# Half of a gated layer's weights through DMA transposes, and a reciprocal shared by two batches from the first group on

## The chip, the cores and the metric

The kernel runs on one core of a Trainium2 chip. The metric is device time in microseconds (us) of one execution. Before the change three runs took 1891.08, 1893.07 and 1893.68 us; the median is 1893.07.

## The reference

Two layers are computed on x (64 batches, 128 steps, 512 features) in 32-bit floats. Layer 0 is a gated recurrence without a matrix in its loop; layer 1 is a GRU whose 128 steps follow one another, conditioned on a vector for each batch.

```python
# layer 0
f = sigmoid(x @ W_f.T + b_f);  i = sigmoid(x @ W_i.T + b_i)
total = f + i + 1e-8;  f, i = f / total, i / total
new = i * (x @ W_h.T + b_h)
lc = cumsum(log(f + 1e-8))          # over time
hidden = cumsum(exp(lc[-1] - lc_before) * new) + exp(lc) * cond
x = x + hidden
# layer 1: gates z and r, state h, with C_* applied to cond
x = x + gru(cond, x)
```

W_f, W_i and W_h are 512 x 512 and are used transposed: the contraction runs over their columns.

## The kernel before, in words

**Groups and chunks.** Layer 0 takes the 64 batches in 16 groups g of four (512 columns: 4 batches of 128 steps), and the 512 outputs in four chunks c of 128 partitions. The loop at L1038 goes over (g, c). For each chunk `chunk_products` (L280) calls `gate` (L219) three times, n = 0, 1, 2 for W_f, W_i, W_h. A gate is four matmuls of 128x512 (L232), one for each 128 of the contraction, into one of two PSUM banks of its kind. ScalarE applies the sigmoid to the first two (L285, L291). VectorE then does the rest of the chunk: `chunk_total` (L319) adds f and i, `chunk_shares` (L322) divides by that sum, `chunk_new` (L374), `chunk_retained` (L385) and `chunk_summed` (L379) are a product and scans over time. The steps of a chunk end within the next one: `chunk_rest` (L400) puts `chunk_weighted` (L393) and `chunk_initial` (L398) of the chunk before behind the sum of the present one, and on GpSimd (POOL) `chunk_first` (L312), `sums_of_chunk` (L278) and `add_hidden` (L253). `add_hidden` also stores the new x to DRAM, as x2d (L261, on the SP queue). `add_eps` (L308) is one more step on ScalarE, between VectorE's L349 and its scans.

**The division.** In group 0 VectorE takes the reciprocal of all 512 sums of a partition (L328). In later groups the reciprocal is shared: batches are paired, the product of two sums is formed (L335, `r`), its reciprocal taken (L337, half as many elements), and multiplied with the other sum of the pair (L339, `over`). `r` and `over` lie in the two PSUM banks of the tag "tp".

**Weights of layer 0.** They come as rows, 12 pieces of 128 outputs by 512 (`load_w_rows`, L91, one for each chunk c and kind n) into `w_rows`. TensorE turns each piece with four transposes (L190) into a "tp" bank, and ScalarE copies it (L191) into W0. The pieces of chunks 0 and 1 are turned while chunk (0,0) runs; in chunks 1 and 2 the three pieces of the following chunk are turned one by one between the gates (`chunk_products`, `w0_transposed`).

**x.** Group 0's x comes as rows and is transposed on TensorE. For later groups another way is used. A float is two 16-bit halves. `x_halves` (L152) issues DMAs that transpose 16-bit elements from DRAM into the tile `held` (L155): the two halves of a float end up in neighbouring partitions. `x_words` (L160) sends them from there, in four DMAs on SP of 64 KB (L166), into a tile `words`, where both halves of a number lie in the same partition. `x_joined` (L171) is one ScalarE copy (L177) that interleaves the halves into xT. There are four sets of words for each group, (u, m) = (0,0), (0,1), (1,0), (1,1), and two `words` buffers (tag "x", which `cond_sb` uses first). The sets of group g+1 are sent and joined during group g, and xT of a group is needed from its first gate on.

**After chunk (1,0)** `conditioning` (L444) loads the three conditioning weights C_r, C_z and C of layer 1 into the tile `cw` (L428, 1 MB each, on SP), which takes the place of `w_rows` (tag "wa"), and multiplies them with the transposed cond (`pv`, 64 matmuls at L473, in both "tp" banks). They stand behind chunk (1,0)'s last gate on TensorE. `bias1` is filled by twelve small DMAs (L448). Layer 1's other weights, w_s and w_x (L435), are loaded in pieces.

**What sets the order.** Instructions passed to `pin` keep the order of the program on their engine: all matmuls, ScalarE, VectorE and POOL work around the change. The DMAs on SP are not pinned; a scheduler places them when the kernel is built, and SP then takes its queue in that order, waiting at each DMA for what it needs. ScalarE's joins, copies and sigmoids are one queue in program order.

Of the kernel before, what the change touches and what calls it, by code (L numbers as in the profile page):

```python
# [10 lines left out]
U16 = mybir.dt.uint16  # L11
# [4 lines left out]
P = 128  # L16
# [3 lines left out]
def kernel(  # L20
# [38 lines left out]
    nc = tc.nc  # L59
    B, S, D = x.shape  # L60
    K = D // P
    GB = 4
    NG = B // GB
# [12 lines left out]
    work = ctx.enter_context(tc.tile_pool(name="work", bufs=1))  # L76
    psum = ctx.enter_context(tc.tile_pool(name="psum", bufs=2, space=PSUM))

    def pin(instruction):
        return tc.keep_in_program_order(instruction)  # L80
# [8 lines left out]
    w_rows = wpool.tile([P, K, 3, D], F32, tag="wa", name="w_rows")  # L89

    def load_w_rows(c, n):  # L91
        nc.sync.dma_start(w_rows[:, c, n, :], (W_f, W_i, W_h)[n][c * P : (c + 1) * P, :])

    x_rows = {}

# [46 lines left out]
    def by_batch(t):  # L142
        return t[:, 1:NP].rearrange("p (b t) -> p b t", t=S1)[:, :, :S]
# [6 lines left out]
    words = {}  # L150
# [20 lines left out]
    def x_joined(g, u, m):  # L171

        if u == m == 0:
            xT[g] = work.tile([P, K, NT], F32, tag="xt", bufs=2, name=f"xT_{g}")
        to = xT[g][:, m * K // 2 : (m + 1) * K // 2, u * NT // 2 : (u + 1) * NT // 2]
        pin(
            nc.scalar.copy(  # L177
                to.bitcast(U16).rearrange("p k (n h) -> p k n h", h=2),
                words.pop((g, u, m)).rearrange("p k h n -> p k n h"),
            )  # L180
        )
# [4 lines left out]
    def transposed(dst, rows, n=P, m=K, copy=nc.scalar.copy):  # L186

        tp = psum.tile([P, m, n], F32, tag="tp", name="tp")
        for k in range(m):
            pin(nc.tensor.transpose(tp[:, k, :], rows[:, k * P : (k + 1) * P], ident[:n, :n]))  # L190
        pin(copy(dst, tp))  # L191
# [11 lines left out]
    W0 = wpool.tile([P, K, 3, K, P], F32, tag="wb", name="W0")  # L203

    xT = {}

    def w0_transposed(c, n, copy=nc.scalar.copy):
        transposed(W0[:, c, n], w_rows[:, c, n, :], copy=copy)

# [9 lines left out]
    def gate(g, c, n):  # L219
        p = psum.tile([P, NT], F32, tag=f"p{n}", name=f"p{n}_{g}_{c}")  # L220

        blocks = [slice(0, NT)]
        if (g, c, n) == (0, 0, 0):
            copies = (nc.vector.tensor_copy, nc.scalar.copy)
            blocks = [slice(tb * P, (tb + 1) * P) for tb in range(K)]
            w0_transposed(0, 0)
            for tb in range(2):
                x_transposed(0, tb, copy=copies[tb % 2])
        for tb, tokens in enumerate(blocks):
            for k in range(K):  # L230
                pin(
                    nc.tensor.matmul(  # L232
                        p[:, tokens],
                        lhsT=W0[:, c, n, k, :],
                        rhs=xT[g][:, k, tokens],
                        start=(k == 0),
                        stop=(k == K - 1),
                    )
                )
            if len(blocks) > 1 and tb + 2 < K:  # L240
                x_transposed(0, tb + 2, copy=copies[tb % 2])
            elif len(blocks) > 1 and tb + 2 == K:
                transposed(biasT, bias0, n=3 * K, m=1)
                w0_transposed(0, 1)
        return p.rearrange(f"{layout(g)} -> p b t", b=GB)
# [34 lines left out]
    def chunk_products(g, c):  # L280

        f, i = fs[c % 2], is_[c % 2]
        fb, ib = by_batch(f), by_batch(i)
        p = gate(g, c, 0)
        pin(nc.scalar.activation(fb, p, AF.Sigmoid, bias=biasT[:, 0, c : c + 1]))  # L285
        if g == 0 and c == 0:
            w0_transposed(0, 2)
        elif g == 0 and c + 1 < K:
            w0_transposed(c + 1, 0)
        p = gate(g, c, 1)  # L290
        pin(nc.scalar.activation(ib, p, AF.Sigmoid, bias=biasT[:, 0, K + c : K + c + 1]))  # L291
        if g == 0 and c == 0:
            transposed(condT, cond_sb, n=B)
            w0_transposed(1, 0)
        elif g == 0 and c + 1 < K:
            w0_transposed(c + 1, 1)
        if g + 1 < NG:
            for u, m in ((), ((0, 0), (0, 1)), ((1, 0),), ((1, 1),))[c]:
                x_joined(g + 1, u, m)
        p = gate(g, c, 2)  # L300
        if g == 0 and c + 1 < K:
            for n in range(1 if c == 0 else 2, 3):
                w0_transposed(c + 1, n)
        return p

    def add_eps(c):
        fb = by_batch(fs[c % 2])
        pin(nc.scalar.activation(fb, fb, AF.Copy, bias=EPS))  # L308
# [13 lines left out]
    def chunk_shares(g, c, meanwhile):  # L322

        h = hidden[g, c]
        hb = by_batch(h)
        if g == 0:
            meanwhile()
            pin(nc.vector.reciprocal(h, h))  # L328
            over = hb
        else:  # L330
            r = psum.tile([P, NT], F32, tag="tp", name=f"r_{g}_{c}")[:, : NT // 2]
            over = psum.tile([P, NT], F32, tag="tp", name=f"over_{g}_{c}")
            pairs = hb.rearrange("p (a b) t -> p a b t", a=2)
            r_ = r.rearrange("p (b t) -> p b t", t=S)
            pin(nc.vector.tensor_tensor(r_, pairs[:, 0], pairs[:, 1], ALU.mult))  # L335
            meanwhile()
            pin(nc.vector.reciprocal(r, r))  # L337
            pin(
                nc.vector.tensor_tensor(  # L339
                    over.rearrange("p (a b t) -> p a b t", a=2, t=S),  # L340
                    pairs[:, ::-1],
                    r_.unsqueeze(1).to_broadcast([P, 2, GB // 2, S]),
                    ALU.mult,
                )
            )
            over = over.rearrange("p (b t) -> p b t", t=S)
        both = fi[c % 2][:, :, 1:NP].rearrange("p n (b t) -> p n b t", t=S1)[:, :, :, :S]
        pin(
            nc.vector.tensor_tensor(  # L349
                both, both, over.unsqueeze(1).to_broadcast([P, 2, GB, S]), ALU.mult  # L350
            )
        )
        add_eps(c)
# [684 lines left out]
    for g in range(NG):  # L1038
        for c in range(K):
            last = g == NG - 1 and c == K - 1  # L1040
            if g + 1 < NG and c == 0:
                x_halves(g + 1, 0)
                x_halves(g + 1, 1)
            elif g + 1 < NG and c < K - 1:
                x_words(g + 1, c - 1, 0)
                x_words(g + 1, c - 1, 1)
            p = chunk_products(g, c)
            meanwhile = chunk_rest(g, c)
            if last:
                meanwhile()  # L1050
                break
            chunk_shares(g, c, meanwhile)
            if g > 0:
                load(4)

            if g >= 2 and (c == 0 or c == 2 and g >= 14):
                subtracts(early_differences, 1)
            if g == NG - 1 and c == 0:
                load_window(0, 1, NG // 2 - 1)
            chunk_new(g, c, p)  # L1060
            chunk_retained(g, c)
            chunk_summed(g, c)
            if (g, c) == (1, 0):
                vs = conditioning()
                w_x = load_weights("w_x", (W_r, W_z, W), "wa")
                w_s = load_weights("w_s", (U_r, U_z, U), "wu")
                v_d = dram.tile([2, SB, Q, 3 * P], F32, name="v_d")
                for s in range(2):
                    nc.sync.dma_start(
                        v_d[s].rearrange("b q e -> q b e"), vs[s].rearrange("p g e -> p (g e)")  # L1070
                    )
                w_inner = wpool.tile([P, 12, 3, P], F32, tag="wi", name="w_inner")
                w_products, outer_differences = outer_weights()
                plain = [n for n in range(7) if OPERANDS[n][1] < 3]
                early_differences = iter(
                    outer_differences
                    + [
                        d
                        for m, n in enumerate(plain[:2])
                        for d in inner_differences(n, [w_inner[:, 4 * m + i] for i in range(4)])  # L1080
                    ]
                )
        if g == NG - 5:
            streams = [Stream(s) for s in range(2)]
            load_window(0, 0)
        if g == NG - 4:
            for f in gathers(0, 0):
                f()
# [105 lines left out]
    for n in range(2):  # L1194
        t = work.tile([P, 5, 3, P], F32, tag="xt", bufs=2, name=f"w_inner{n}")
# [14 lines left out]
    for t in range(LEAD + 1, S):  # L1210
        n = order[-1][1] + 1
# [70 lines left out]
    n = 0  # L1282
# [44 lines left out]
```

## Time and profile before

| | |
|---|---|
| runs, median | 1893.07 us |
| profiled execution | 1891.55 us, span 1889.8 us |
| gate of four matmuls (chain of waits) | 3.44 us |
| four transposes of one weight piece (chain of waits) | 0.44 us |
| ScalarE copy of a transposed piece, L191 | 0.58 us |
| ScalarE join, L177 | 1.16 us |
| sum of chunk 1, 2, 3 of group 0 starts on VectorE | 29.09, 40.77, 51.95 us |
| last gate of chunk (1,0) ends, `pv` starts | 64.86, 67.47 us |

The profile is that of one execution. Times count from the start of the span. "Busy" is the time in which an engine worked; the chain of waits follows the work that ended last back from the end, at each step to what released it. For a DMA the profile has the time that its issue took on the queue of the engine (SP here), and the time from issue to landing.

### The profile page before, as it was taken

To read this page: it belongs to the slowest core of one execution; us is meant where nothing else is said; L and a number is where in the kernel's file an instruction comes from. 1 tells how busy PE (TensorE), PEld (TensorE's weight loads), DVE (VectorE), ACT (ScalarE), POOL (GpSimd) and SP (SyncE) were. 2 spreads that over 40 slices of the span, in tenths; PEclk is the share of its full clock that TensorE was granted. 3 is DMA by queue.
4 is the path that set the end of the run, shared out by engine and by line. 5 is a ranking of instruction groups with operands and counts; after the bars stand their busy time and mean duration, and the time that the engine had idled before them with its cause. 6 is when DMAs were issued, how large, how long until landed. Compare 5 with 4: busy or idle time off the path is not lost.

```text
span 1889.8 us, 62579 instructions
## 1 busy us (share of the span) xinstructions
PE 1870.6 (99%) x24921; PEld 1078.2 (57%) x24921; DVE 1487.8 (79%) x3438; ACT 722.0 (38%) x1880; POOL 864.1 (46%) x1544
## 2 busy tenths in 40 slices
PE   9999999999999999999999999999999999999998
PEld 5444444444444445566666666666666666666667
DVE  5799999999999976567777777777777777777776
ACT  3232223222232223244444444444444444444434
POOL 1233332333323335355555565555565565655650
PEclk9999999999999999999999999999999999999999
DMA  7755433443342222234344344444443443443343
GB/s 182 175 116 122 80 71 74 89 83 78 73 84 59 46 61 54 79 83 132 98 123 124 103 133 119 104 137 110 101 137 101 119 129 99 126 122 104 111 111 77
DMA packets 366563, 195.02 MB, mean 103 GB/s; under 512 B 225396, under 2 KB 351872, under 8 KB 366272
## 3 DMA queue, kind: packets, MB, share of 16 engines
q1 hardware_dynamic: 365992, 190.95, 40.7%
q8 instruction: 196, 3.21, 0.8%
q14 instruction: 95, 0.78, 0.2%
q10 hardware_dynamic: 280, 0.08, 0.0%
HBM read 78.24 MB, written 81.13 MB: 84 GB/s over the span
## 4 chain that ended last, share of the span: by engine, by line
PE 96%; DVE 2%; DMA 0%; issue 0%; ACT 0%; POOL 0%; ACTq 0%; DVEq 0%; SPq 0%; POOLq 0%
PE g L473 36%; PE p L232 34%; PE r L599 14%; PE r12a L599 4%; PE shared L599 4%; PE r12b L599 3%; PE gz L473 1%; PE tp L190 0%; PE pv L473 0%; DVE fi L918 0%; DMA x<-in_x_dram 0%; DVE fi L919 0%; DVE h L328 0%; DMA out_dram<-o_last 0%; DVE W L701 0%
## 5 line engine op out<-in xcount | busy, mean ns | idle before, releaser
L232 PE MATMUL p<-xT,W 128*128 128x512 f32 (+1 forms) x1560 | 661.8, 586 | 0.1
L232 PEld LDWEIGHTS p<-xT,W 128*128 128x128 f32 x1560 | 293.4, 190 | 361.6 <-issue 359.4
L473 PE MATMUL g<-w_s,h 128*32 128x256 f32 (+1 forms) x8128 | 481.1, 373 | 3.5 <-DVE h L970 2.4
L473 PEld LDWEIGHTS g<-w_s,h 128*32 128x32 f32 x8128 | 311.9, 110 | 168.0 <-issue 79.1
L473 PEld LDWEIGHTS g<-w_s,fi 128*32 128x32 f32 x8128 | 224.0, 109 | 111.3 <-issue 52.7
L473 PE MATMUL g<-w_s,fi 128*32 128x128 f32 x8128 | 276.2, 273 | 4.5 <-DVE fi L918 3.1
L918 DVE TENSOR_TENSOR fi<-fi,h 128x64 f32<-128x64 f32 (+1 forms) x494 | 109.2, 221 | 187.7 <-ACT fi L914 187.0
L981 POOL TENSOR_TENSOR h<-h,x 128x128 f32<-128x128 f32 x242 | 122.2, 505 | 225.9 <-DVE h L970 213.0
L312 POOL COPY first<-condT 128x4 f32<-128x4 f32 x64 | 12.4, 194 | 463.4 <-DVE h L398 428.4
L914 ACT ACTIVATE fi<-g 128x128 f32<-128x128 f32 x254 | 70.4, 277 | 328.4 <-PE g L473 324.2
L929 POOL TENSOR_SCALAR fi<-fi 128x128 f32<-128x128 f32 x240 | 72.4, 301 | 258.5 <-DVE fi L918 252.1
L701 DVE TENSOR_TENSOR W<-r,W 128x384 f32<-128x384 f32 x315 | 170.1, 540 | 10.2 <-POOL held L807 0.5
L308 ACT ACTIVATE fi<-fi 128x512 f32<-128x512 f32 x64 | 40.3, 630 | 335.5 <-DVE fi L349 335.2
L953 ACT ACTIVATE h<-g 128x128 f32<-128x128 f32 x256 | 71.1, 278 | 239.1 <-PE g L473 239.1
L919 DVE STREAM_TRANSPOSE fi<-fi 128x64 f32<-128x64 f32 (+1 forms) x494 | 122.2, 247 | 22.5
L965 DVE TENSOR_TENSOR h<-h,fi 128x128 f32<-128x128 f32 (+1 forms) x264 | 81.7, 309 | 57.2 <-ACT h L953 57.0
L253 POOL TENSOR_TENSOR x<-xT,h 128x512 f32<-128x512 f32 x63 | 122.8, 1950 | 4.9
L930 POOL TENSOR_TENSOR fi<-fi,h 128x128 f32<-128x128 f32 x240 | 111.1, 463 | 20.0
L599 PE MATMUL r<-w_inner,held 128*32 128x384 f32 x1080 | 115.3, 486 | 0.0
L807 POOL TENSOR_TENSOR held<-held 128x128 f32<-128x128 f32 x240 | 112.9, 483 | 3.6
L966 DVE TENSOR_TENSOR h<-h,fi 128x128 f32<-128x128 f32 (+1 forms) x264 | 91.6, 347 | 27.1 <-DVE h L965 1.8
L337 DVE RECIPROCAL r<-r 128x256 f32<-128x256 f32 x59 | 102.5, 1737 | 0.0
(164 smaller groups left out, 2751.9 us busy)
## 6 DMA issues: line engine op xcount, KB each, us to landing
shares<-W SPq DMA_DIRECT2D x240, 192.0 KB, 2.0
xz<-shares SPq DMA_DIRECT2D x476, 48.0 KB, 1.9
whole_v<-shares SPq DMA_DIRECT2D x476, 48.0 KB, 2.0
x2d<-x SPq DMA_DIRECT2D x63, 256.0 KB, 3.9
words<-held SPq DMA_DIRECT2D x240, 64.0 KB, 2.1
out_dram<-o SPq DMA_DIRECT2D x240, 64.0 KB, 1.8
xw_None<-x2d SPq DMA_DIRECT2D x56, 256.0 KB, 3.4
w_rows<-in_L_cond_W_f_dram SPq DMA_DIRECT2D x4, 256.0 KB, 6.1
```

Source lines behind the costliest of these rows:

```text
L232: nc.tensor.matmul(p[:, tokens], lhsT=W0[:, c, n, k, :], rhs=xT[g][:, k, tokens], start=(k == 0), stop=(k == K - 1),)
L253: nc.gpsimd.tensor_tensor(x2.rearrange("p (t b) -> p t b", b=GB)[:, ts], xT[g][:, c, :].rearrange(f"{layout(g)} -> p t b", b=GB)[:, ts], b ...
L337: pin(nc.vector.reciprocal(r, r))
L473: nc.tensor.matmul(p[q * SB : (q + 1) * SB], lhsT=lhsT(k), rhs=part(wk, q), start=(start and k == 0), stop=(stop and k == len(w) - 1), ski ...
L599: nc.tensor.matmul(self.bank(bank)[q * SB : (q + 1) * SB], lhsT=a[:, q * SB : (q + 1) * SB], rhs=w_, start=start, stop=True, skip_group_ch ...
L701: pin(nc.vector.tensor_tensor(dst, r, other, ALU.add))
L807: pin(nc.gpsimd.tensor_tensor(*a))
L918: pin(nc.vector.tensor_tensor(rh[:, e], r[:, e], h_[:, e], ALU.mult))
L919: pin(nc.vector.transpose(rhT[:, e], rh[:, e]))
L930: pin(nc.gpsimd.tensor_tensor(r, r, h_, ALU.mult))
L966: pin(nc.vector.tensor_tensor(h[:, e], hh[:, e], r[:, e], ALU.add))
L981: nc.gpsimd.tensor_tensor(hh.rearrange("p (k b) -> p k b", b=SB), hT.rearrange("p (k b) -> p k b", b=SB), x_of(self, t), ALU.add,)
```

## The change

Three things change, all in group 0. (1) The six weight pieces of chunks 2 and 3 are loaded by transposing DMAs of 16-bit halves, the way of x in later groups; each piece then goes through four words DMAs (`w0_words`) and one ScalarE join (`w0_joined`). Their transposes on TensorE and copies on ScalarE go. (2) During group 0 one list, `joins`, holds the order of all ten sets: W(2,0), W(2,1), W(2,2), x(0,0), x(0,1), W(3,0), W(3,1), W(3,2), x(1,0), x(1,1). They share the two `words` buffers. Two sets are sent ahead of chunk 1; each join then sends the next set. The joins are spread over the gates of chunks 1 to 3. (3) Chunks 1 to 3 of group 0 use the shared reciprocal.

```diff
     def load_w_rows(c, n):
-        nc.sync.dma_start(w_rows[:, c, n, :], (W_f, W_i, W_h)[n][c * P : (c + 1) * P, :])
+        rows = (W_f, W_i, W_h)[n][c * P : (c + 1) * P, :]
+        if c < 2:
+            nc.sync.dma_start(w_rows[:, c, n, :], rows)
+        else:
+            nc.sync.dma_start_transpose(halves_of_w(c, n), rows.bitcast(U16))
+
+    def halves_of_w(c, n):
+        return w_rows[:, c, n, :].bitcast(U16).rearrange("p (b n) -> p b n", n=P)
...
+    def w0_words(c, n):
+        t = work.tile([P, K, 2, P], U16, tag="x", bufs=2, name=f"words_w_{c}_{n}")
+        words["w", c, n] = t
+        for h in range(2):
+            for j in range(2):
+                nc.sync.dma_start(
+                    t[j * P // 2 : (j + 1) * P // 2, :, h], halves_of_w(c, n)[h::2, j::2]
+                )
+
+    def w0_joined(c, n):
+        pin(
+            nc.scalar.copy(
+                W0[:, c, n].bitcast(U16).rearrange("p k (n h) -> p k n h", h=2),
+                words.pop(("w", c, n)).rearrange("p k h n -> p k n h"),
+            )
+        )
+
+    joins = [(w0_words, w0_joined, 2, n) for n in range(3)]
+    joins += [(x_words, x_joined, 1, 0, 0), (x_words, x_joined, 1, 0, 1)]
+    joins += [(w0_words, w0_joined, 3, n) for n in range(3)]
+    joins += [(x_words, x_joined, 1, 1, 0), (x_words, x_joined, 1, 1, 1)]
+    to_part = list(joins)
+
+    def parted(n):
+        for f, _, *a in to_part[:n]:
+            f(*a)
+        del to_part[:n]
+
+    def joined(n):
+        for _, f, *a in joins[:n]:
+            f(*a)
+            parted(1)
+        del joins[:n]
...
         if g == 0 and c == 0:
             w0_transposed(0, 2)
-        elif g == 0 and c + 1 < K:
-            w0_transposed(c + 1, 0)
+        elif g == 0:
+            joined((0, 1, 2, 1)[c])
...
             w0_transposed(1, 0)
-        elif g == 0 and c + 1 < K:
-            w0_transposed(c + 1, 1)
-        if g + 1 < NG:
+        elif g == 0:
+            joined((0, 1, 1, 1)[c])
+        elif g + 1 < NG:
             for u, m in ((), ((0, 0), (0, 1)), ((1, 0),), ((1, 1),))[c]:
                 x_joined(g + 1, u, m)
         p = gate(g, c, 2)
-        if g == 0 and c + 1 < K:
-            for n in range(1 if c == 0 else 2, 3):
+        if g == 0 and c == 0:
+            for n in range(1, 3):
                 w0_transposed(c + 1, n)
+        elif g == 0:
+            joined((0, 2, 1, 0)[c])
...
-        if g == 0:
+        if g == 0 and c == 0:
             meanwhile()
             pin(nc.vector.reciprocal(h, h))
...
-            elif g + 1 < NG and c < K - 1:
+            elif g == 0 and c == 1:
+                parted(2)
+            elif 0 < g < NG - 1 and c < K - 1:
                 x_words(g + 1, c - 1, 0)
                 x_words(g + 1, c - 1, 1)
```

## The prediction

> **What bounds the kernel.** I read the page first, then the chain of waits of the first 75 us, then what waits around the one place where the chain leaves TensorE.
>
> ```profile
> span 1889.8 us, 62579 instructions
> PE 1870.6 (99%) x24921; PEld 1078.2 (57%) x24921; DVE 1487.8 (79%) x3438; ACT 722.0 (38%) x1880; POOL 864.1 (46%) x1544
> ...
> PEclk9999999999999999999999999999999999999999
> ...
> PE 96%; DVE 2%; DMA 0%; issue 0%; ACT 0%; POOL 0%; ACTq 0%; DVEq 0%; SPq 0%; POOLq 0%
> ```
>
> TensorE is busy 99% of the span at full clock and carries 96% of the chain. So 1 us less TensorE work, or 1 us less idle on it, is 1 us of the time, and a wait it has to sit out is given back nowhere. One such wait exists early; the chain of waits between 50 and 75 us shows it (start, length, what):
>
> ```profile
> 54.59 3.29 DVE h L328
> ...
> 65.03 1.67 DVE r L337
> 66.70 0.02 issue
> 66.72 0.71 DVE over L339
> 67.43 0.04 issue
> 67.47 5.37 PE pv L473 x64
> ```
>
> TensorE ends its last product of chunk (1,0) at 64.86 and then idles 2.61 us, until VectorE's `over` (L339) is written and `pv` may start. `pv` also reads `cw`, the 3 MB of layer 1's conditioning weights. Its rows, and SP's time line:
>
> ```profile
> L428 SPq DMA_DIRECT2D cw<-in_L_cond_C_r_dram x1: 2225/2225/2225, 47.5 to 47.5; - x1
> ...
>   DVE over L339: 6.1, 2
> ...
> DMA to landing us min/median/max: 9.1/9.9/10.7
> ```
>
> ```profile
> 47.05 0.43 SPq L261 DMA_DIRECT2D x2d<-x  x1
> 47.52 2.23 SPq L428 DMA_DIRECT2D cw<-in_L_cond_C_r_dram  x1
> 49.79 0.51 SPq L428 DMA_DIRECT2D cw<-in_L_cond_C_z_dram  x1
> 50.34 0.51 SPq L428 DMA_DIRECT2D cw<-in_L_cond_C_dram  x1
> 57.70 0.37 SPq L261 DMA_DIRECT2D x2d<-x  x1
> ```
>
> `cw` is issued at 47.5; the second of its DMAs lands at 49.8 + 10.7 = 60.5, and the DMA share falls off by 61. So all of `cw` takes about 13.3 us from its first issue, and today has 6.5 us to spare. Keep this margin in mind: `cw` lies in the buffer of `w_rows`.
>
> **Part 1: TensorE and ScalarE work taken away.** Six groups of four transposes (L190 on `w_rows`, chunks 2 and 3) go. In the chain each stands as 0.44 us between gates: 6 x 0.44 = 2.6 us off TensorE. ScalarE loses six copies of 0.58 us and gains six joins; the join of x with the same 1024 16-bit elements a partition takes 1.16 us (L177). ScalarE is busy 38%, so the work itself, 6 x 0.58 = 3.5 us, costs nothing; its order does (part 3).
>
> **Part 2: the shared reciprocal** in chunks 1 to 3 of group 0. Before, L328 to L349 starts 3.47 us apart (54.51 to 57.98). In the shared form of (1,0): r 0.33 (63.47 to 63.80), reciprocal 1.77 (64.95 to 66.72), product 0.80 (66.72 to 67.52): 2.90. It saves 0.57 us a chunk on VectorE. TensorE without transposes takes 3 x 3.44 = 10.3 us a chunk and VectorE 9.8 (10.3 between its starts at 51.95 and 62.26, less 0.5), so VectorE could just follow.
>
> Parts 1 and 2 alone would give up to 2.6 + 0.5 = 3 us.
>
> **Part 3: what is added and moved.** In SP's queue six plain loads become transposing DMAs; 24 small DMAs (`words_w`) come in; and in the built order of the changed kernel's SP queue `cw` stands later: behind the last set of words of x, four transposing DMAs for group 2 and the store x2d(0,2), where before it stood right behind x2d(0,1) (47.05). SP takes its queue in order, so `cw` now waits for POOL's x2 of chunk (0,2), which that store sends: 57.68 today (L253, 56.16 + 1.52). That alone takes away 57.7 - 47.05 = 10.6 us of lead where 6.5 were spare.
>
> The `words` tiles (W and x alike) take turns in two buffers, ten sets one after another, and set n is sent only when ScalarE has joined set n-2. ScalarE joins in program order, with the sigmoids between. So I follow the chain by hand, with these rows: a gate 3.44; a join 1.15; a set of four words DMAs 0.65 apart, its last landing 2.12 after issue, thus 4.07 from the first issue to landing; a bias load 0.47; a transposing DMA 1.3 (median of L155's issues).
>
> - The ten transposing DMAs start at 7.13, land at about 1.3 us each behind the last plain load (12.81): the tenth at about 26, and SP is free near 23.9.
> - W(2,0): sent 23.9, landed 27.9, joined 29.1; wanted by TensorE at 31.2. W(2,1): sent 26.5, joined 31.7; wanted 34.6. Both in time.
> - Twelve bias loads and one of `w_s` now come in one row: 12 x 0.47 + 0.45, SP is free at 35.3. W(2,2): landed 39.3, joined 40.5; wanted at 38.1. **Stall 2.4.**
> - x(0,0): sent 37.9, joined 43.1. x(0,1), behind the store x2d(0,0) and W(2,2)'s join: sent 41.1, landed 46.0, joined 47.2. W(3,0), after x(0,0)'s join: sent 43.7, landed 47.7, joined 48.9; wanted at 44.0. **Stall 4.9.**
> - Behind W(3,0)'s join waits the sigmoid of (0,2,1), done by 49.5; for that waits VectorE's chunk 2 (49.6; before 40.8).
> - W(3,1): sent 47.2 (x(0,1)'s join), joined 52.5, on time (52.4). W(3,2): joined 55.1, wanted 56.0.
> - x(1,0) is joined at 58.7. x(1,1), behind x2d(0,1) at 55.6: landed 61.1, joined 62.3; TensorE reaches it at 61.1. **Stall 1.2.** TensorE ends (1,0) at 70.9 (before 64.9: 2.4 + 4.9 + 1.2 - 2.6 = 5.9).
> - VectorE, from 49.6 at 9.8 a chunk, starts chunk (1,0) at 69.7 and writes `over` at 74.6 (before 67.4). POOL's x2 of (0,2) follows L398 in chunk 3 (62.2) by 3.1 (54.59 to 57.68 before): 65.3.
> - x2d(0,2) at 65.4, `cw` at 65.8, landed 13 us later: **78.4 to 79.1**. `pv` starts there instead of at 67.47: **+11 to +11.6**.
>
> From `pv` on the queues stand to each other as before, with TensorE full. Sum: profiled execution 1891.55 (its span 1889.8 and 1.75 around it) + 11.3 = 1902.9. The median of the runs is 1893.07, 1.5 above the profiled one, so 1904.4 by that. I count all cases from half way, 1892.3: 1892.3 + 11.3 = 1903.6, said as 1903.5.
>
> **What no row shows** (ends worked through the same chain). A words DMA of W has elements of 256 bytes where that of x has 512. Below: the issue of a bias load, 0.45, landing 1.8: `pv` at 75.7, +8.2. Above: twice, 1.3 as a transposing issue, landing 3.5 as `w_s`: 92.7, +25. I take the row of x, same bytes and same tiles. The transposing DMAs in a row of ten: 0.95 (256 KB at the 270 to 290 GB/s that the DMA view shows from 30 to 31.9 while one flows) to 1.5 (21.12 to 22.60, landing of the last two of today's first four): `pv` at 78.1 to 80.0, +10.6 to +12.5.
>
> The Trainium skill ("DMA: Bandwidth & Descriptors", Specifications) asks for 512 B or more a descriptor, which speaks against the 256-byte words; its section "Why small descriptors are slow (HBM only)" exempts SBUF to SBUF. The latter puts the loss at 27% for 256 B: of the 0.3 us that 64 KB take at 220 GB/s, an estimate of 0.1 us a DMA by the first rule, and nothing by the exemption. The same page (Latency and other measured facts) has 261 GB/s for a transposing DMA, an estimate of 1.0 us each; the rows here, issue 1.3, are slower, and would set the sum.
>
> **Rivals.** (A measurement of this kernel can tell about 0.2%, 3.8 us, from no change.)
>
> - Forecast, 0.62: joins late and `cw` last: 1899 to 1908.
> - Words of W dearer, 0.13: SP's row of 24 costs up to twice: at 0.9 an issue `pv` starts at 82.4 (+15), at 1.3 at 92.7 (+25): 1908 to 1917. For it: half the element size. Against: issue times of 0.4 to 0.6 for DMAs of very different counts.
> - Only `cw` late, 0.15: words arrive before they are wanted, no gate stalls. Then x2 of (0,2) at 57.7 - 2.9 = 54.8, `cw` at 55.2 + 13.3 = 68.5, `pv` 1.0 later than now: 1893.3, between 1890 and 1897. For it: W(2,0) and W(2,1) are in time; against: the bias loads ahead of W(2,2), and two buffers for ten sets.
> - The other side, 0.04: no gate stalls and `cw` lands within 9.4 us (before 64.6, when VectorE is done), as the first of its DMAs did in 9.1. Then the 2.6 and 0.5 us are kept: 1889.2. It decides at `cw` landing; against: 3 MB at the 386 GB/s seen from 55 to 60 us are 8 us without the start.
> - Anything else, 0.06, mostly slower.
>
> The range that holds the forecast and the near parts of its neighbours: 1894 to 1912. Faster 0.03 (below 1888.5: the low half of the fourth case and a little of the last), same 0.16 (the third, the rest of the fourth), slower 0.81.
>
> **What would show it.** Right: no L190 work on chunks 2 and 3; TensorE idle before (0,2,2) and (0,3,0) with a release by ScalarE's join, whose own wait ends with `words`; `cw` issued after 62 us; TensorE idle before `pv` by a DMA, not by `over`; the rest of the span shifted and unchanged. Wrong: `cw` issued near 55, or `pv` released by VectorE, or gates without gaps; then one of the lower cases holds. A longer issue than 0.65 for W's words gives the upper one.

## The result and the profile after

Five runs of each on the same chip: 1909.45 us (1908.52 to 1909.90) with the change, 1893.24 (1891.08 to 1893.88) before. The ratio is 1.0085, 95% interval 1.0075 to 1.0096: 16.2 us slower. The forecast was +11.3 and 1903.5, within 1894 to 1912.

The page of the changed kernel's profile (the same lines as were shown of before):

```profile
span 1906.3 us, 62581 instructions
...
PE 1872.9 (98%) x24897; PEld 1077.0 (56%) x24897; DVE 1488.0 (78%) x3444; ACT 725.8 (38%) x1880; POOL 866.0 (45%) x1544
...
PEclk9899999999999999999999999999999999999999
...
PE 93%; issue 3%; DVE 2%; DMA 1%; POOL 1%; SPq 0%; ACT 0%; ACTq 0%; DVEq 0%; POOLq 0%
```

24 TensorE instructions fewer, and yet 2.3 us more busy time; and the row of the granted clock has an 8 in its second slice (47.7 to 95.3 us), where before it had a 9. Both point to a slower clock somewhere in 48 to 95 us. DMA and POOL now have 1% each of the chain of waits. Its early part shows why (start, length, what):

```profile
64.10 1.53 POOL x L296
65.63 0.02 issue
65.65 0.37 SPq L304
66.02 0.04 issue
66.06 1.33 SPq L473
...
68.20 12.37 DMA cw<-in_L_cond_C_dram
80.57 0.14 issue
80.71 7.02 PE pv L518 x64
```

Where the chain before ran through VectorE's `over` into `pv`, it now runs from POOL's x2 of chunk (0,2) over the store x2d(0,2) (L304) to `cw` (L473), whose last DMA lands at 80.57. `pv` starts 13.2 us later than before (67.47) and takes 7.02 us instead of 5.37.

SP's time line between 35 and 70 us shows what went ahead of `cw`:

```profile
35.07 2.58 SPq L220 DMA_DIRECT2D words_w<-w_rows  x4
...
44.18 8.50 SPq L220 DMA_DIRECT2D words_w<-w_rows  x12
52.87 2.54 SPq L173 DMA_DIRECT2D words<-held  x4
56.13 0.39 SPq L304 DMA_DIRECT2D x2d<-x  x1
56.69 2.90 SPq L173 DMA_DIRECT2D words<-held  x4
59.64 5.44 SPq L162 DMA_TRANSPOSE held<-in_x_dram  x4
```

Before, `cw` stood right behind x2d(0,1); here that store leaves at 56.13 and nine more DMAs follow before `cw`. TensorE's time line (start, length, what, instructions, and in brackets the idle time before and what ended it):

```profile
21.25 17.33 PE L275 MATMUL p<-xT,W 128*128 128x512 f32 x40
40.52 3.70 PE L275 MATMUL p<-xT,W 128*128 128x512 f32 x8 [1.94 <-ACT W L227]
49.66 22.70 PE L275 MATMUL p<-xT,W 128*128 128x512 f32 x48 [5.44 <-ACT W L227]
80.71 7.02 PE L518 MATMUL pv<-cw,condT 128*32 128x384 f32 x64 [8.35 <-DMA cw<-in_L_cond_C_dram]
```

The rows of transposes between the gates are gone: five gates (40 records) run in one row. Then three waits: for W(2,2) before gate (0,2,2), for W(3,0) before (0,3,0), and for `cw`. The six gates from 49.66 take 22.70 us; the same row before took 20.77 (44.09 on). ScalarE's time line shows the joins that end the first two waits, and what ended the joins' own waiting:

```profile
39.31 1.16 ACT L227 COPY W<-words_w 128x1024 uint16<-128x1024 uint16 x1 [7.74 <-DMA words_w<-w_rows]
...
48.45 1.16 ACT L227 COPY W<-words_w 128x1024 uint16<-128x1024 uint16 x1 [1.70 <-DMA words_w<-w_rows]
49.52 0.68 ACT L334 ACTIVATE fi<-p,biasT 128x512 f32<-128x512 f32 x1
```

ScalarE had nothing to do for 7.74 and 1.70 us: the words came late, not ScalarE. The last of these lines is the sigmoid of (0,2,1), which had to wait behind the join of W(3,0).

Stretches of 2 us (busy time of PE, PEld, DVE, ACT, POOL; then the granted clock, DMA share, GB/s):

```profile
50.00:52.00 2.00, 2.00 (x3) 0.83 (x3) 1.77 (x4) 1.07 (x2) 0.00 (x0) 0.50 0.41 98
52.00:54.00 2.00, 2.00 (x4) 0.79 (x3) 2.00 (x2) 0.29 (x1) 0.92 (x2) 0.66 0.29 70
...
80.00:82.00 2.00, 1.29 (x10) 0.51 (x14) 0.00 (x0) 0.00 (x0) 0.00 (x0) 0.50 0.42 87
82.00:84.00 2.00, 2.00 (x20) 0.77 (x16) 0.00 (x0) 0.00 (x0) 0.00 (x0) 0.50 0.28 74
84.00:86.00 2.00, 2.00 (x32) 0.86 (x28) 0.56 (x1) 0.00 (x0) 0.00 (x0) 0.98 0.35 98
```

Behind the second and the third wait TensorE runs at half clock: 20 `pv` matmuls in a full stretch against 32 at 0.98. That is the new term that no step of the prediction had. Against before, up to `pv`'s end (87.73, before 72.84):

| | us |
|---|---|
| transposes of six pieces gone | -2.62 |
| a later start (the gate at 21.25 stood at 20.86) | +0.39 |
| waits before (0,2,2) and (0,3,0): 1.94 + 5.44 | +7.38 |
| six gates slower (22.70 - 20.77) | +1.93 |
| starts and ends of rows of gates at the two waits | +0.39 |
| wait before `pv` longer (8.35 - 2.61) | +5.74 |
| `pv` slower (7.02 - 5.37) | +1.65 |
| sum; measured 14.89 | +14.86 |

The later start of 0.39 is scatter: over the profiles of all kernels here this gate starts between 20.74 and 21.78, and at 21.54 in the run with the shared reciprocal alone, which changes nothing ahead of it. The sums of the following groups on VectorE stand 14.88 to 15.16 us later all through layer 0 (groups 2 to 15). The spans differ by 16.5, so another 1.6 come together in layer 1. That rest can't be laid to the change: in the profiles of the experiments it lies between -2.0 (before with `cw` late) and +1.8 (all words apart).

### The profile page after: what moved, and what is told of

It is laid out like the page before. It is cut to its first block, busy times and chain, and to the rows that moved or that the text cites. A ratio compares the mean times of both kernels' runs of the same rounds, so it can differ in the third digit from the quotient of the medians.

```text
span 1906.3 us, 62581 instructions
## 1 busy us (share of the span) xinstructions
PE 1872.9 (98%) x24897; PEld 1077.0 (56%) x24897; DVE 1488.0 (78%) x3444; ACT 725.8 (38%) x1880; POOL 866.0 (45%) x1544
## 3 DMA queue, kind: packets, MB, share of 16 engines
q8 instruction: 196, 3.21, 0.7%
## 4 chain that ended last, share of the span: by engine, by line
PE 93%; issue 3%; DVE 2%; DMA 1%; POOL 1%; SPq 0%; ACT 0%; ACTq 0%; DVEq 0%; POOLq 0%
PE g L518 35%; PE p L275 32%; PE r L644 14%; PE shared L644 3%; PE r12a L644 3%; PE r12b L644 3%; DMA cw<-in_L_cond_C_dram 1%; PE gz L518 0%; PE pv L518 0%; SPq L1069 0%; POOL x L296 0%; DVE W L746 0%; POOL h L321 0%; DVE fi L963 0%; DMA x<-in_x_dram 0%
## 5 line engine op out<-in xcount | busy, mean ns | idle before, releaser
L382 DVE RECIPROCAL r<-r 128x256 f32<-128x256 f32 x62 | 107.9, 1740 | 0.0
```

## The experiments

Theory: the loss is waiting on TensorE (late joins, `cw` last), and half clock behind the waits. Rivals: the DMA transposes and words as such are too dear (then no order of them helps); or the shared reciprocal, or the place of `cw` alone, makes the difference. Each median is told with its ratio to runs of before on the same chip. "Shift" is how much later layer 0's sums of groups 4 to 14 start on VectorE than in before's profile.

**The shared reciprocal alone**, in the kernel before:

```diff
-        if g == 0:
+        if g == 0 and c == 0:
             meanwhile()
             pin(nc.vector.reciprocal(h, h))
```

> The kernel before with one part of the change alone: chunks 1 to 3 of group 0 use the shared reciprocal; weights as before. My theory (the shared reciprocal shortens VectorE's chain to pv and nothing else): over of chunk (1,0) is written 0.5 us earlier, because only the last of the three savings is not absorbed by VectorE's waits on the sigmoids, and pv starts at about 66.9 where it was 67.47; time 0.5 us less, 1892.5 to 1893. Rival (it costs: its two PSUM banks are wanted by the transposes of chunks 2 and 3 at the same time): TensorE idles in chunks 1 to 3 of group 0 by some 1 us each, time 1894 to 1897.

1892.24 us, ratio 1.0001 (0.9991 to 1.0010). The expected 0.5 us is smaller than this interval, so the time can't settle it; the time lines can. VectorE's has the starts of chunks (0,3) and (1,0):

```profile
52.63 0.70 DVE L319 SCALAR_TENSOR_TENSOR h<-fi 128x517 f32<-128x517 f32 x1 [1.49 <-ACT fi L291]
62.93 0.70 DVE L319 SCALAR_TENSOR_TENSOR h<-fi 128x517 f32<-128x517 f32 x1 [0.67 <-ACT fi L291]
```

What VectorE saves, it waits for the next chunk's sigmoid, that is, for TensorE (before the change it waited 0.78 before chunk (0,3), and not at all before (1,0)). `pv` starts 2.87 us behind the last gate, where it was 2.61: no earlier. A saving on an engine that the next chunk keeps waiting isn't one.

**`cw` early**, in the changed kernel: `cw` in a tile of its own, sent once W(3,2) is joined, ahead of the transposing DMAs and x2d(0,2):

```diff
+            if (g, c) == (0,3):
+                cw = load_weights("cw", (C_r, C_z, C_h), "wc", after=made[("w", 3, 2)])
...
-        cw = load_weights("cw", (C_r, C_z, C_h), "wa", by_part=False)
```

> The changed kernel with cw in the buffer of a tile that is not used yet (that of the differences of layer 1's weights), and its loads tied to the join of W(3,2): in SP's queue they stand right behind the last words of x, ahead of the transposing DMAs for group 2 and of x2d(0,2). My theory (cw's place in the queue costs the last 5.5 us ahead of pv, and the long idle time there half of TensorE's clock): cw issued near 60, landed by 74, pv released by over at 75.2 instead of 80.7, at full clock (5.4 us instead of 7.0): 7.2 us less than the changed kernel, 1902. Gate stalls before (0,2,2) and (0,3,0) stay as they are. Rival (cw is late because the DMA engines are full, not because of its place): pv still waits for a DMA until 79 or later, time 1907 or more.

1903.09 us, ratio 1.0056 (1.0040 to 1.0073), as the theory had it. `cw` is issued from 60.8 and landed by 72.2. TensorE's last gates and `pv`:

```profile
50.76 22.31 PE L276 MATMUL p<-xT,W 128*128 128x512 f32 x48 [5.49 <-ACT W L228]
75.94 5.37 PE L520 MATMUL pv<-cw,condT 128*32 128x384 f32 x64 [2.87 <-DVE over L385]
```

`pv` is released by `over` again, as before the change, and runs at 5.37. The shift is 8.47 us instead of 14.89: `cw`'s place, with the clock drop that it brings, costs 6.4 of the change's loss. The gates' waits stay (3.23 and 5.49, against 1.94 and 5.44: the first words of W are sent 1.1 us later in this execution).

**Own words**, in the changed kernel: each of W's six sets of words in a buffer of its own, so that none waits for a join:

```diff
-        t = work.tile([P, K, 2, P], U16, tag="x", bufs=2, name=f"words_w_{c}_{n}")
+        t = words_of_w[:, 3 * (c - 2) + n]
```

> The changed kernel with a words buffer of its own for each of the six weight pieces (in a tile that is not used yet); x's words keep the two buffers. The built order then sends nearly all words ahead of the bias loads; cw stays behind x2d(0,2). My theory (the gate stalls come from two buffers and from the bias loads between the sets): no stall before (0,2,2), under 1 us before (0,3,0); chunk 2 starts on VectorE near 43 instead of 50.2, cw lands near 73, pv starts there, still at half clock: 7 to 9 us less than the changed kernel, 1900 to 1903. Rival (SP's 40 words DMAs at 0.65 us each are too many by themselves): the stall before (0,3,0) stays over 4 us and the time over 1906.

1906.68 us, ratio 1.0076 (1.0060 to 1.0091): only 2.8 us less than the change by the medians, and the expected 1900 to 1903 missed; the rival's time came, but not its stall of over 4 us at (0,3,0). The joins did come earlier: TensorE waits 1.15 and 0.93 us at the gates, and their clock stays full. But the built order of SP's queue is another (first fence), and TensorE pays at `pv` (second):

```profile
59.14 2.28 SPq L495 DMA_DIRECT2D bias<-in_L_cond_b_r_dram  x4
...
64.78 0.38 SPq L306 DMA_DIRECT2D x2d<-x  x1
...
66.45 0.44 SPq L475 DMA_DIRECT2D cw<-in_L_cond_C_r_dram  x1
```

```profile
79.13 8.07 PE L520 MATMUL pv<-cw,condT 128*32 128x384 f32 x64 [13.80 <-DMA cw<-in_L_cond_C_dram]
```

The twelve bias loads moved behind the words, from 28.8 to 59.1, and stand between the transposing DMAs and `cw`. So `cw` leaves no earlier (66.45) although VectorE's sum of (0,2) is 6.4 us earlier: nearly all of the gain at the gates is waited out before `pv`. The two losses aren't a sum; they stand one behind the other on the way to one event.

**Filler**, in the changed kernel: TensorE is kept busy with matmuls that nobody reads, six ahead of gate (0,3,0) and nine ahead of `pv`; `cw` tied behind x2 of (0,2). They add work and leave nothing out:

```diff
+        if (g, c, n) == (0, 3, 0):
+            filled(p, 6)
...
+        filled(psum.tile([P, NT], F32, tag="p0", name="filler"), 9)
```

> The changed kernel with matmuls that nothing reads put into TensorE's two long waits: six of 128x512 before gate (0,3,0) and nine before pv; cw is tied to POOL's x2 of (0,2), so that it keeps its place behind x2d(0,2). Nothing that is waited for comes earlier. My theory (idle for some 5 us, TensorE is granted half its clock for about 4 us after): gates from (0,3,0) on run at 3.44 us from the first, pv takes 5.4 instead of 7.0; since pv waits for cw, only the 1.6 us in and behind pv show in the time: 1907.5 to 1908.5. Rival (the matmuls after the waits are slow for another reason, as DMA traffic or reads of freshly written tiles): pv still takes 7.0 and the time is as that of the changed kernel, 1909 to 1910, or longer by the work added.

1909.98 us, ratio 1.0091 (1.0076 to 1.0106), not the time expected. Gates (0,3,0) to (1,0,2), and `pv`:

```profile
51.67 20.76 PE L286 MATMUL p<-xT,W 128*128 128x512 f32 x48
...
83.36 6.77 PE L533 MATMUL pv<-cw,condT 128*32 128x384 f32 x64 [3.21 <-DMA cw<-in_L_cond_C_dram]
```

Without idle time ahead of them the six gates take 20.76 instead of 22.70: idleness is what slows them, not where they stand or what runs beside them. But gate (0,2,2) here ran at half clock behind its wait of 2.26 us (5.40 instead of 3.70), so the filler began late and ended later than the join it bridged (the gates start 2.0 us later than in the changed kernel), `cw` left 3 us later, behind three words DMAs and x2d(0,2) at 67.89, and `pv` still had 3.21 us of idle time before it and half clock. So for the clock at the gates the verdict is clear; as a time the run tells nothing.

**Before with `cw` late**: nothing of the change, only `cw` tied behind x2 of (0,2):

```diff
-        cw = load_weights("cw", (C_r, C_z, C_h), "wa", by_part=False)
+        cw = load_weights("cw", (C_r, C_z, C_h), "wa", by_part=False, after=added_of[0, 2])
```

> The kernel before, unchanged but for cw's loads, which are tied to POOL's x2 of (0,2): in SP's queue they move from behind x2d(0,1) to behind x2d(0,2), their place in the changed kernel. My theory (cw's place alone costs): cw issued near 58, landed near 71, TensorE idle from 64.9 to 71 before pv, then at half clock: pv ends near 78 instead of 72.8, time 1897 to 1899. Rival (the margin of cw is larger than read from the landings): pv is still released by over at 67.5, time as before.

1899.26 us, ratio 1.0037 (1.0023 to 1.0051), 0.3 us above the theory's range.

```profile
72.21 7.70 PE L477 MATMUL pv<-cw,condT 128*32 128x384 f32 x64 [7.38 <-DMA cw<-in_L_cond_C_dram]
```

The place of `cw` alone costs 7.1 us of shift: 4.8 more waiting (7.38 against 2.61) and 2.3 of half clock. No DMA transpose of weights is needed for that.

**Weights' words first**, on top of `cw` early: in the list of joins all six pieces of W ahead of x.

```diff
+    joins = [(w0_words, w0_joined, c, n) for c in (2, 3) for n in range(3)]
+    joins += [(x_words, x_joined, 1, u, m) for u in range(2) for m in range(2)]
```

> The kernel with cw early (the second experiment) with one more edit: the list of the ten sets has the six weight pieces first and the four sets of x behind them; two buffers as before. My theory (the stall before (0,3,0) comes from x's two sets ahead of W(3,0) in the two-buffer chain and ScalarE's order): W(3,0) is joined near 43, stall before (0,3,0) under 1 us, that before (0,2,2) as it is; VectorE starts chunk 2 near 48 instead of 50 to 51, pv starts near 73 instead of 75.9 and the time is 1899 to 1901. Rival (what delays VectorE's chunk 2 is only ScalarE's joins ahead of the sigmoid, whichever they are): the stall goes but pv does not start earlier, time 1902 to 1904.

1905.19 us, ratio 1.0071 (1.0057 to 1.0085), where 1899 to 1901 was expected, and 1902 to 1904 by the rival: neither number came.

```profile
62.08 13.29 PE L274 MATMUL p<-xT,W 128*128 128x512 f32 x24 [6.85 <-ACT xT L184]
78.22 6.83 PE L518 MATMUL pv<-cw,condT 128*32 128x384 f32 x64 [2.86 <-DVE over L383]
```

The wait before (0,3,0) is gone, and 6.85 us of waiting stand before chunk (1,0), now for x's words, sent from 47.4 to 60.5 with the first DMA of `cw` among them (53.56). VectorE's chunk (0,2) starts at 50.02, hardly earlier than the 51.32 of the run with `cw` early: its sigmoid (it starts at 49.31) stands on ScalarE right behind the join of W(3,2), which begins at 48.24 after a wait of 1.68 for words. So the rival's mechanism, joins ahead of the sigmoid, is the one that held. In both orders that were tried, two buffers for ten sets make one of them late.

**All words apart**: `cw` early, W first, buffers of their own for W's six sets and for the last two of x, and the joins spread otherwise over the gates.

```diff
+    own_words = wpool.tile([P, 8, K * 2 * P], U16, tag="wi", name="own_words")
...
+        if g == 1 and u == 1:
+            t = own_words[:, 6 + m].rearrange("p (k h n) -> p k h n", k=K // 2, h=2)
```

> A version meant to be good: the changed kernel with cw early, weight pieces first, a buffer of its own for each of the eight sets of the weights and of x's second half, and joins spread so that none stands ahead of a sigmoid whose words come later. My theory (with words in time and cw in time the change gives back what it takes off TensorE): no gate stall over 0.5 us, (1,0) ends near 62.5 instead of 64.9, pv starts near 65 and is released by over; time 2 to 2.5 us less than before, 1890 to 1891.5. Rival (cw, issued near 51 in two parts with the words ahead of it, lands after 68): no better than before, 1893 to 1896.

1894.66 us, ratio 1.0016 (1.0007 to 1.0025).

```profile
21.78 41.59 PE L278 MATMUL p<-xT,W 128*128 128x512 f32 x96
67.29 7.96 PE L522 MATMUL pv<-cw,condT 128*32 128x384 f32 x64 [3.92 <-DMA cw<-in_L_cond_C_dram]
```

All twelve gates from 21.78 run in one row without a wait: for these gates the DMA transposes and words as such are fast enough, and the rival "too dear in any order" is out. But `cw`, issued at 51.84, 52.98 and, as the second issue held SP for 4.37 us, 57.41, lands only at about 67.2, 0.9 us behind `over` (66.28). `pv` waits 3.92 us (2.61 before) and then runs at half clock, 2.59 us more than the 5.37. That eats the 2.62 us of transposes, and the expected 1890 to 1891.5 was missed for it.

**All words apart, `pv` later**: the same with `conditioning` and what follows it behind the gates of chunk (1,1):

```diff
-            if (g, c) == (1, 0):
...
+            if (g, c) == (1, 1):
                 vs = conditioning(cw)
...
```

> The version above with layer 1's conditioning (pv and the loads behind it) moved in the program from behind chunk (1,0) to behind the gates of chunk (1,1), so that TensorE has those 10.3 us of work while VectorE writes over of (1,0). My theory (the remaining wait of some 2.5 us before pv is the last one of this stage): TensorE has no idle over 0.5 us between 10 and 100 us; time 2 to 2.7 us less than the version above, 1887.5 to 1889.5. Rival (VectorE falls behind: it waits for pv before r of (1,1), and the PSUM banks then hold TensorE in chunk (1,2) or (1,3)): the wait comes back there, time as the version above or longer.

1896.98 us, ratio 1.0024 (1.0015 to 1.0033), where 1887.5 to 1889.5 was expected.

```profile
73.84 5.37 PE L522 MATMUL pv<-cw,condT 128*32 128x384 f32 x64
...
107.41 7.92 PE L278 MATMUL p<-xT,W 128*128 128x512 f32 x14 [3.92 <-ACT xT L188]
```

`pv` has no wait and full speed, but group 2's gates wait 1.50 and 3.92 us for joins, since the built order puts the last eight words DMAs of x for group 2 at 95.28, behind twelve bias loads (79.0 to 85.9), weights and the store x2d at 94.81. That is neither the theory nor its rival, which had VectorE and the PSUM banks hold TensorE.

**Before with `pv` later**: nothing of the change; `conditioning` and what follows it behind the gates of (1,1), as in the last diff.

> The kernel before with one thing moved: the conditioning products (pv) and what follows them come behind the gates of chunk (1,1), not behind those of (1,0). None of the change's other parts is in it. Theory (TensorE's idle time is the price, and it can be covered): over of (1,0) is written at 67.4 and cw lands near 61 to 70, both while the gates of (1,1) run (64.9 to 75.2), so pv starts at 75.2 without a wait at 5.37 us and the 2.61 us of idle time are gone: 1889 to 1890. Rival (as in the run with all words and the later conditioning): pv, moved, puts words of x of group 2 later in SP's queue, and TensorE waits for their join at group 2's first gates: 1892 to 1896.

1888.76 us (11 runs), ratio 0.9981 (0.9972 to 0.9990): faster by 3.8 us by the medians, a little more than expected; the spans of the profiled executions differ by the expected 2.6. Of the 29 runs of before beside it, 16 have a mean granted clock of 1.000 and a median of 1891.75; the other 13 are lower in clock and have 1893.64. That fits half clock behind before's own wait in a part of its executions (last section), which the profiled one doesn't have; the traces of the others weren't kept.

```profile
44.33 31.07 PE L232 MATMUL p<-xT,W 128*128 128x512 f32 x72
75.32 5.37 PE L473 MATMUL pv<-cw,condT 128*32 128x384 f32 x64
```

Nine gates and `pv` in one row: the 2.61 us before `pv` are gone, the shift is -2.45. Here the built order keeps group 2's words early, so the wait of the run before doesn't appear.

**The change with `cw` early and `pv` later.** The two edits above together.

> The changed kernel with cw sent behind the join of W(3,2) (as in the run with cw early) and pv moved behind the gates of (1,1). Theory: the two stalls before gates (0,2,2) and (0,3,0) and the slow clock behind the second stay (about 3.2, 5.5 and 2), pv has no wait and runs in 5.37 us, so the shift after pv is 8.5 less 2.9 less 0: +5.5, 1897 to 1900. Rival (words of group 2 late, since they stand behind cw and four transposing DMAs in SP's queue): a new wait at group 2's first gates of 2 to 5 us, 1900 to 1904.

1898.22 us, ratio 1.0029 (1.0018 to 1.0039), within the theory's range.

```profile
50.28 33.80 PE L276 MATMUL p<-xT,W 128*128 128x512 f32 x72 [3.78 <-ACT W L228]
84.01 5.37 PE L520 MATMUL pv<-cw,condT 128*32 128x384 f32 x64
```

The shift is 6.24 us: waits of 3.03 and 3.78 at the gates, 1.70 and 2.73 of half clock behind them (5.40 for the gate that took 3.70 in the changed kernel, 33.80 for the 31.07 of the run before), less 2.62 and 2.61: 6.0. The parts aren't those of the theory (3.2, 5.5 and 2): gate (0,2,2) ran at half clock too, and what it lost by that shortened the wait behind it. What is left of the change's loss is late joins and their clock.

**Half of the change**: only chunk 3's three pieces by DMA transposes, with three buffers of their own, sent at once; chunk 2 by TensorE as before; x's words as before; the shared reciprocal in.

```diff
-        if c < 2:
+        if c < 3:
             nc.sync.dma_start(w_rows[:, c, n, :], rows)
...
-        t = work.tile([P, K, 2, P], U16, tag="x", bufs=2, name=f"words_w_{c}_{n}")
+        t = own_words[:, n].rearrange("p (k h n) -> p k h n", k=K, h=2)
```

> Half of the change: only chunk 3's three weight pieces come by transposing DMAs and words, sent at once into three buffers of their own; chunk 2 is transposed by TensorE as before; x's words are sent as before; the shared reciprocal is in. Theory (the loss is late joins and a late cw, not the DMA transposes themselves): no gate waits for a join; in the built order cw stands around x2d(0,1) as before (its second and third DMA behind it), so it is issued by 49 to 57 and lands by 62 to 70; TensorE saves 3 x 0.44 = 1.3; pv waits for over (near 66) or for cw. 1890.5 to 1893.5. Rival (every form of the change makes cw late): cw lands after 72 and pv with it: over 1896.

1895.58 us, ratio 1.0017 (1.0009 to 1.0026), 2 us above the theory's range and below the rival's.

```profile
68.76 7.01 PE L508 MATMUL pv<-cw,condT 128*32 128x384 f32 x64 [4.74 <-DMA cw<-in_L_cond_C_dram]
```

No gate waits for a join (right), and `cw` leaves at 53.4, 54.8 and 59.1 and lands near 68.6, within the expected 62 to 70. What was missed is again the clock: 4.74 us of idle time bring `pv` to 7.01.

**Half of the change, `pv` later.**

> The half of the change of the run beside it, with pv moved behind the gates of (1,1). Theory: 1.3 off TensorE and the 2.6 of idle time covered: 1892 less 3.9: 1887.5 to 1889.5, faster than both kernels, if cw lands by 73.5. Rival: cw's three DMAs are spread between words of group 2 and x2d(0,2) and land after 74, or group 2's words come late: 1890 to 1895.

1888.80 us (11 runs), ratio 0.9979 (0.9971 to 0.9988): faster than both kernels, and no faster than before with `pv` later (1888.76), within the theory's range.

```profile
43.26 31.17 PE L265 MATMUL p<-xT,W 128*128 128x512 f32 x72 [0.28 <-ACT W L228]
74.36 5.37 PE L508 MATMUL pv<-cw,condT 128*32 128x384 f32 x64
```

`pv` starts 0.96 us earlier than in that run: the 1.3 us of three pieces' transposes, less a wait of 0.28 for a join. Layer 0's shift is -3.41 against -2.45, but the spans are 1886.9 and 1887.2; two thirds of that 1 us are gone by the end of layer 1, and the medians don't tell the two apart.

## Why the prediction was right, and which terms were not

- **TensorE's transposes, -2.6.** Right: -2.62.
- **Shared reciprocal, up to -0.5.** Measured alone: nothing on the way to `pv`, as VectorE then waits for the sigmoid. The step said "VectorE could just follow"; it could, and then stands idle. Before's rows had this: the sigmoid ahead of chunk (1,0) ended at 62.21, and VectorE's sum started at 62.26. The sum uses the step only in VectorE's 9.8 us a chunk (9.55 measured).
- **Words of W at x's price (0.65 an issue).** Right: 12 in a row took 8.50 us with the waits for joins in them, 8 took 5.37; the landing has a median of 2.2 us, x's words 2.1. The upper case of dearer words is out.
- **The chain of joins.** W(2,0) joined at 29.41 (29.1 said), W(2,2) 40.47 (40.5), W(3,0) 49.61 (48.9), W(3,1) 52.29 (52.5). Stalls 1.94 and 5.44 (2.4 and 4.9 said; 7.38 against 7.3, so the sum fits better than its parts). W(2,1) had its join at 31.57 (31.7).
- **A stall of 1.2 at (1,0,0).** Not there: x(1,1) was joined at 62.35 (62.3 said), but the gates ahead of it ran 1.93 us slower, and TensorE reached this one only at 61.89 (61.1 said).
- **x2 of (0,2), x2d(0,2), `cw`'s issue.** 65.63, 65.65 and 66.06; said 65.3, 65.4 and 65.8. The link that decides the loss was right to 0.3 us, and two runs show it from both sides: put `cw` forward and 6.4 us come back, put it back in the kernel before and 7.1 are lost.
- **`cw` lands 13 us after its first issue.** Too short here: 14.5 (66.06 to 80.57). From the first issue to landing it took 11.5 with `cw` early (60.3 to 71.8 in the run with `pv` later too), 13.8 in the kernel before with `cw` late, 15.4 with all words apart. What else the DMA engines and SP then had to do differs between these runs; which of it sets the time wasn't tried by itself. This term was 1.2 to 1.5 us too small (13 to 13.3 said), and its start 0.3 late.
- **"From pv on the queues stand to each other as before".** This is the step that failed for `pv` itself and, earlier, for the gates: each was priced at its old duration. With the half clock behind the waits, 1.9 at the gates and 1.65 at `pv` come in. The former didn't reach `cw`: that hangs on VectorE, which works from 50.23 on without idle time (9.55 from chunk (0,2) to chunk (0,3); 9.8 said), and only shortened the wait before `pv`. The 69.7 that the prediction has for chunk (1,0) isn't 49.6 and twice 9.8, which is 69.2; it was 69.74, with 0.36 of waiting for the sigmoid, and nothing in the sum rests on it. From `pv`'s end on the step held for layer 0: a shift of 14.9 to 15.2 in all groups.

Sum by these: +11.3 said; `pv` started 13.2 later, +1.65 for its own slowness is 14.9, and +1.6 came together in layer 1, which is within the scatter told above. The mechanism was right and the size 30% short, by a later landing and a clock that before's trace (1.00 everywhere, also behind its 2.61 us of idle time) gave no reason to expect.

## What to carry to other kernels

When work is taken off the engine that bounds a kernel and is given to a queue, follow the queue to the next transfer that stands behind it: here 2.6 us of transposes were paid with 13 us at a load that had nothing to do with them. Price a wait on TensorE as the wait and, from some 4 us on, 1.4 to 2.8 us of half clock behind it; between 2.1 and 4 us that depends on where the wait falls in the clock's windows (next section), so it can differ between two executions of one kernel. Where one such wait is left, look for independent work to put in front of it (here the next chunk's gates were at hand, and moving `pv` by one chunk made the kernel before 0.2% faster). A transfer freed earlier by more buffers is only earlier if the built order of its queue lets it, so read that order again after each edit.

## What the runs showed of the hardware that was not expected

The granted clock of TensorE falls to 0.50 behind idle time, and the work that follows runs at half rate for 2.9 to 5.5 us (80.71 to 84.10 in the changed kernel, 67.29 to 72.58 with all words apart). Idle time before, and what followed:

| idle time before, us | clock behind it |
|---|---|
| 0.93, 1.15, 1.50, 1.94, 2.53, 2.61, 2.87 (`cw` early), 3.23 | full |
| 2.26 (filler), 2.86, 2.87 (reciprocal alone), 3.03, 3.21 | half |
| 3.78, 3.92, 4.74, 5.44, 5.49, 6.85, 7.38, 8.35, 13.80 | half |

So between 2.3 and 3.2 us it went either way, the same 2.87 in two kernels once so and once so, and from 3.78 on it always fell. What decides is where the wait lies. In each trace any two changes of the granted clock are a whole number of times 3.41 us apart (in the changed kernel 46.55, 53.38, 77.27 and 84.10: 2, 7 and 2 times). So it changes only at the ends of windows of 3.41 us that follow one another through the whole execution, wherever the program stands. Counted over the 14 traces (behind their first 8 us, where the records begin), it fell at the end of each window in which TensorE had been idle for 2.10 us or more, and at none with 1.90 or less. It came back at the end of the first window with at most 0.53 us of idle time; with 1.31 or more it stayed at half. The 2.61 us of before lay across two windows, the 2.87 of the run with the reciprocal alone fell into one, and so did the 2.26 of the filler run, where the clock fell 0.59 us after the gate had begun (stretch, TensorE's busy time, granted clock, DMA share, GB/s):

```profile
62.70:66.12 3.42, 2.16 (x6) 1.00 0.27 70
66.12:69.53 3.41, 2.06 (x28) 1.00 0.39 103
```

```profile
65.39:68.80 3.41, 0.55 (x9) 1.00 0.30 83
68.80:72.22 3.42, 3.42 (x28) 0.50 0.49 134
```

```profile
38.46:41.87 3.41, 1.15 (x4) 1.00 0.40 105
```

The Trainium skill ("TensorE: Matmul & The Clock Gate", Part 1) has half rate after an idle window of about 3.4 us that runs freely and doesn't start anew with the kernel. The traces agree with the length of the window and with its running freely. They differ in how idle it has to be: 2.10 us of the 3.41 were enough, and there the measurement decides. The prediction's own rows had TensorE idle for some 8 us before `pv` (70.9 to 78.4 or more), which holds a whole such window wherever it begins. So half rate behind that wait could have been priced ahead of the result.

SP's own issues can become long while `cw` is under way: with all words apart the second DMA of `cw` held SP for 4.37 us, where the first took 0.54 and the third 0.50, and what was next in its queue had to wait for it. In three more kernels the second took 4.26 to 5.32 us, in the other ten 0.5 to 1.0; what sets this wasn't tried.
